# 14 of 49 node tiles of a top-1 expert layer through slots sorted by expert, and gathers handed out by a count of TensorE's work

## The chip, the cores and the metric

The kernel runs on one core of one Trainium2 chip. The metric is the device time of one execution in microseconds (us). The kernel before was timed 11 times: median 2865.29 us, from 2860.51 to 2869.4. The profile shows one execution more.

## What is computed

There are 6250 nodes with 256 features and 100,000 weighted edges, sorted by destination. Each of two layers has a part that adds over edges (gnn) and a part of experts (ffn), and each part adds its result to x. In layer 0 every node goes through all 8 experts, weighted by a softmax. In layer 1 each node goes through one of 32 experts only:

```python
x = x + L0_gnn(layernorm(x)); x = x + L0_ffn(layernorm(x))
# L1_gnn
h = layernorm(x) @ weight                      # 256 x 256
x = x + segment_sum(edge_val * h[edge_src], edge_dst) + bias
# L1_ffn, xf = layernorm(x)
idx = argmax(xf @ router_w.T + router_b)       # one of 32 experts for each node
h = relu(xf @ W1[idx] + b1[idx])               # 256 -> 64
x = x + relu(h @ W2[idx] + b2[idx])            # 64 -> 256
```

All of it is float32. x stays in SBUF, as 49 tiles of 128 nodes (X).

## The kernel before, in words

**Stages.** First the edges are sorted (to about 390 us); then comes layer 0 with its dense experts, and from about 1797 us layer 1. The change is in layer 1, apart from one fill in layer 0.

**Columns.** Edges are worked off in columns of 128. Layer 1 has 782, of which the first 64 (NE) are already done at the end of layer 0; 718 are left. `columns1` gives, for a column, a gather of 128 rows of h1 from DRAM (`gather`, L201, an indirect DMA that POOL issues), a scaling on ACT (L230) and a remainder on DVE (L231) into a tile m, a one-hot matrix s of destinations for three columns on DVE (L222), and one matmul that adds the column into its destinations (L277). Every 16 columns a tile of nodes is complete: its sums are put together on DVE, turned on PE (L209) and multiplied by the weight (L214), and added to X (L215). That takes up to LAG = 10 more steps of the generator. Buffers: 23 for gathered rows, 12 for m, 5 for s.

**Dense experts of layer 1.** The tiles are taken in blocks: 3, then 11 blocks of 4, then 2. `begin1` normalizes and turns a block's tiles (L340), computes the router (L973) and a mask that is negative and huge for every expert but the node's own. Two experts make a chunk of 128 hidden features, so there are 16 chunks. `hidden1` multiplies the turned block by a chunk of W1 (L1000) and adds the mask (L1003); ACT applies the relu (L1005). `outs1` multiplies by the chunk of W2 and adds up in PSUM (L1016). So every node goes through all 32 experts, and 31 of its results are zero. `end1` adds the result to X and writes the block (L1023, L1027).

**Order.** The order is written out by hand. A block can begin when all columns of its tiles are summed. `Stream.upto` emits columns up to a given number; `aheads` spreads them evenly over the half chunks, so that the columns of the next block are done some chunks before it begins. The engines work through their own queues in order and wait on semaphores.

**Layer 0, for the fill.** `small1` runs in the third last block of layer 0, at about 1525 us. It loads the router's weights and biases; b2 is loaded from SP into b2f, a tile with one buffer (tag hs), and split on DVE into three parts in bf16 (L803 to L809).

Of the kernel before, what the change touches and what calls it, by code (L numbers as in the profile page):

```python
# [11 lines left out]
I32 = mybir.dt.int32  # L12
# [32 lines left out]
LN_EPS = 1e-5  # L45
BN_EPS = 1e-3
# [3 lines left out]
def gnn_ffn_kernel(ctx: ExitStack, tc: tile.TileContext, a, out):  # L50
# [40 lines left out]
    h1 = dram.tile([NT * P, D], F32, name="h1")  # L91

# [143 lines left out]
    def columns1(pool, psum, js, h, idx, w, bufs):  # L236
# [6 lines left out]
        def summed(q, acc):  # L243
# [15 lines left out]
            else:  # L259
# [3 lines left out]
                sT = pool.tile([P, 2, P], F32, tag="sT", name="sT", bufs=2)  # L263
# [96 lines left out]
    ramp = [3] + [NB] * 11 + [2]  # L360
    blocks1 = [list(range(sum(ramp[:b]), sum(ramp[:b + 1]))) for b in range(len(ramp))]
# [273 lines left out]
    with tc.tile_pool(name="layer0", bufs=1) as wp, tc.tile_pool(name="outs0", bufs=1, side="right") as wo_pool, \  # L635
# [159 lines left out]
        def small1():  # L795


            nc.sync.dma_start(rw, a["router_t"].rearrange("(k p) e -> p k e", p=P))
# [150 lines left out]
        for part in firsts:  # L949
            next(part)  # L950
# [5 lines left out]
    with tc.tile_pool(name="layer1", bufs=1, reuse_waits="tile") as wp, \  # L956
# [8 lines left out]
        def begin1(pool, tiles):  # L965

            n = len(tiles)
            nw = n * P
            nT = norm_t(pool, psum, tiles)
            pl = psum.tile([P, NB, NX1], F32, tag="tr", name="pl", bufs=1)  # L970
            for j in range(n):
                for k in range(2):
                    nc.tensor.matmul(pl[:, j, :], nT[:, k, j * P:(j + 1) * P], rw[:, k, :],  # L973
                                     start=(k == 0), stop=(k == 1))
# [9 lines left out]
            nc.vector.tensor_tensor(g, g, m[:, :, None].to_broadcast([P, n, NX1]), OP.is_equal)  # L984
            hots = work.tile([P, NB, P // NX1, NX1], F32, tag="hots", name="hots", bufs=1)
# [10 lines left out]
        def hidden1(pool, block, c):  # L996
# [7 lines left out]
            hm = pool.tile([P, NB * P], F32, tag="hm", name="hm", bufs=4)  # L1004
# [14 lines left out]
        def end1(pool, tiles, py):  # L1019
            n = len(tiles)  # L1020
            o = pool.tile([P, NB, D], F32, tag="hs", name="o", bufs=2)
            for j, t in enumerate(tiles):
                nc.vector.scalar_tensor_tensor(o[:, j, :], py[:, j, :], 0.0, X[:, t, :], op0=OP.max, op1=OP.add)  # L1023
            t = tiles[0]
            m = min(N - t * P, n * P) // P
            if m:
                nc.sync.dma_start(out[t * P:(t + m) * P, :].rearrange("(t p) d -> p t d", p=P), o[:, :m, :])  # L1027
            if m < n:
                nc.sync.dma_start(out[(t + m) * P:, :], o[:NLAST, m, :])

        with tc.tile_pool(name="flow1", bufs=1, reuse_waits="tile") as flow:

            sums = Stream(columns1(flow, psum, range(NE, NREAL), h1, src_c, val_c, (5, EW + 6, 12, 4)))
            cum = [0] + [min(CS * (2 * tiles[-1] + 2) + CS // 2, NREAL) + LAG - NE for tiles in blocks1[1:]]
# [91 lines left out]
```

## Time and profile before

| | |
|---|---|
| the profiled execution's own time | 2863.55 us |
| its span, first to last instruction | 2861.8 us |
| granted TensorE clock, mean | 0.975 |
| busy: PE, PEld, DVE, ACT, POOL | 2654.3, 1728.1, 1993.6, 1601.3, 1883.9 us |
| gathers of layer 1 (L201, src_c) | 718, issued from 1792.8 to 2741.8 us |
| the last column's matmul (L277) begins | 2784.8 us |
| the last matmul (L1016) | in a group from 2852.61 us |
| the last DMA is issued (L1029) | 2855.46 us |

Busy times are sums over an engine's instructions. Lines of a timeline give the start, the duration, engine, source line and operation, and in brackets how long the engine was idle before and what ended it. A line of a table by stretches gives the busy time and the number of instructions of PE, PEld, DVE, ACT and POOL in this order, then the granted clock, the share of the DMA engines and GB/s. PE is TensorE's matmuls, PEld its loads of weights, DVE VectorE, ACT ScalarE, POOL GpSimd, SP SyncE; a name with q is the engine's sequencer, which issues DMAs too. A float32 matmul of the program is two instructions in the trace.

### The profile page before, as it was taken

The numbers are of one execution on the slowest core, as the hardware profiler recorded it, in microseconds if no ns is written. First come the engines' busy times: TensorE is split into PE (matmuls) and PEld (weight loads), VectorE is DVE, ScalarE is ACT, GpSimd is POOL, SyncE is SP. The second block draws the span as 40 slices with busy tenths as digits, with TensorE's granted clock in tenths as the row PEclk, the third lists the DMA queues.
The fourth block names the chain that finished last, engine by engine and source line by source line (L and its number), as shares of the span: only waits on it lengthen the run. The fifth ranks groups of instructions, "written<-read, shape, count | busy, mean of one in ns | idle before, by whom it ended". The sixth has DMA issues, their size and how long they took to land.

```text
span 2861.8 us, 36648 instructions
## 1 busy us (share of the span) xinstructions
PE 2654.3 (93%) x10178; PEld 1728.1 (60%) x10238; DVE 1993.6 (70%) x4968; ACT 1601.3 (56%) x3741; POOL 1883.9 (66%) x1883
## 2 busy tenths in 40 slices
PE   5888848899999999999999998889999999999998
PEld 2444426765666666666666665556666666666666
DVE  8999987788868777766756646566666666666630
ACT  7777737655555555555554545455555555555532
POOL 4666657777766666666665526777777777777720
PEclk9999978999999999999999999899999999999999
DMA  4000033333333233233332214233333333333310
GB/s 152 19 19 19 19 135 97 102 102 101 92 97 93 86 100 93 84 96 96 94 86 78 84 41 147 86 106 102 105 109 109 107 108 103 106 107 109 109 43 12
DMA packets 120835, 254.30 MB, mean 89 GB/s; under 512 B 31477, under 2 KB 68169, under 8 KB 120617
## 3 DMA queue, kind: packets, MB, share of 16 engines
q0 software_dynamic: 77520, 211.78, 25.7%
q1 hardware_dynamic: 31672, 32.42, 3.4%
q10 hardware_dynamic: 11424, 7.63, 0.8%
q8 instruction: 84, 1.38, 0.2%
q14 instruction: 135, 1.10, 0.1%
HBM read 232.48 MB, written 19.25 MB: 88 GB/s over the span
## 4 chain that ended last, share of the span: by engine, by line
PE 63%; DMA 8%; DVE 6%; issue 6%; ACT 2%; POOL 1%; ACTq 0%; POOLq 0%; DVEq 0%; another core or an unknown queue 0%
PE ph L764 19%; PE py L776 10%; PE py L1016 9%; PE ph L1000 9%; PE acc L707 5%; PE acc L277 5%; DMA g<-h,src_c 4%; DMA g<-h,idx 3%; DVE m L231 1%; ACT m L230 1%; POOL g L201 1%; PE ph L214 1%; PE tr L340 1%; PE ph L1003 1%; PE pl L973 1%
## 5 line engine op out<-in xcount | busy, mean ns | idle before, releaser
L201 POOL DMA_INDIRECT g<-h,idx x833 | 858.2, 1030 | 397.3 <-DVE m L231 195.5
L201 POOL DMA_INDIRECT g<-h,src_c x718 | 728.7, 1015 | 233.8 <-issue 103.0
L230 ACT ACTIVATE m<-g,w 128x256 fp32r<-128x256 f32 x833 | 370.8, 500 | 259.8 <-PE acc L707 161.4
L230 ACT ACTIVATE m<-g,val_c 128x256 fp32r<-128x256 f32 x718 | 348.2, 503 | 269.8 <-PE acc L277 142.3
L767 ACT ACTIVATE hT<-ph,shift,scale 128x512 f32<-128x512 f32 (+3 forms) x480 | 329.3, 696 | 292.8 <-PE ph L764 284.7
L231 DVE SCALAR_TENSOR_TENSOR m<-g,val_c,m 128x256 fp32r<-128x256 f32 x718 | 336.3, 483 | 206.3 <-ACT m L230 202.1
L231 DVE SCALAR_TENSOR_TENSOR m<-g,w,m 128x256 fp32r<-128x256 f32 x833 | 377.7, 477 | 28.7 <-ACT m L230 27.9
L764 PE MATMUL ph<-nT,w 128*128 128x512 f32 (+3 forms) x960 | 374.8, 526 | 20.4 <-ACT hT L767 20.2
L1016 PE MATMUL py<-w,hm 128*128 128x256 f32 x1568 | 385.8, 384 | 2.4 <-ACT hm L1005 2.2
L776 PE MATMUL py<-wo,hT 128*128 128x256 f32 x1568 | 377.8, 385 | 7.2 <-DVE X L778 4.6
L1000 PE MATMUL ph<-nT,w 128*128 128x512 f32 (+2 forms) x832 | 378.9, 576 | 0.0
L764 PE MATMUL ph<-hT,w 128*128 128x512 f32 (+3 forms) x960 | 366.8, 517 | 0.7 <-ACT hT L767 0.7
L707 PE MATMUL acc<-m,s 128*128 128x512 f32 x833 | 313.6, 482 | 38.8 <-DVE scale L663 27.6
L776 PEld LDWEIGHTS py<-wo,hT 128*128 128x128 f32 x1568 | 291.9, 191 | 75.5 <-DVE X L778 22.0
L277 PE MATMUL acc<-m,s 128*128 128x512 f32 x782 | 333.2, 500 | 1.2 <-DVE m L231 1.2
L1016 PEld LDWEIGHTS py<-w,hm 128*128 128x128 f32 x1568 | 291.4, 193 | 52.4 <-ACT hm L1005 4.3
L222 DVE TENSOR_TENSOR s<-col,dl 128x384 fp32r<-128x384 f32 (+1 forms) x294 | 155.0, 528 | 194.8 <-PE acc L707 194.4
L764 PEld LDWEIGHTS ph<-nT,w 128*128 128x128 f32 x960 | 174.1, 196 | 166.5 <-issue 116.5
L1005 ACT ACTIVATE hm<-ph,b 128x512 f32<-128x512 f32 (+2 forms) x208 | 136.9, 659 | 208.3 <-PE ph L1003 152.3
L764 PEld LDWEIGHTS ph<-hT,w 128*128 128x128 f32 x960 | 174.8, 191 | 121.4 <-issue 91.9
L707 PEld LDWEIGHTS acc<-m,s 128*128 128x128 f32 x833 | 159.7, 195 | 104.2 <-issue 50.9
L1000 PEld LDWEIGHTS ph<-nT,w 128*128 128x128 f32 x832 | 158.7, 193 | 102.2 <-issue 81.8
(254 smaller groups left out, 3341.2 us busy)
## 6 DMA issues: line engine op xcount, KB each, us to landing
g<-h,idx POOLq DMA_INDIRECT x833, 2.8
g<-h,src_c POOLq DMA_INDIRECT x718, 2.8
h<-hs SPq DMA_DIRECT2D x25, 256.0 KB, 2.1
X<-in_x_dram SPq DMA_DIRECT2D x12, 512.0 KB, 8.2
out_dram<-o SPq DMA_DIRECT2D x11, 512.0 KB, 3.4
h<-hs SPq DMA_DIRECT2D x9, 512.0 KB, 3.0
w<-in_L_ffn_W_dram ACTq DMA_DIRECT2D x2, 2048.0 KB, 7.9
wo<-in_L_ffn_Wo_dram ACTq DMA_DIRECT2D x1, 2048.0 KB
```

The lines of the kernel that those rows point to most:

```text
L201: nc.gpsimd.indirect_dma_start(out=g, out_offset=None, in_=h, in_offset=bass.IndirectOffsetOnAxis(ap=idx, axis=0))
L222: nc.vector.tensor_tensor(s[:, :n], col[:, None, :].to_broadcast([P, n, P]), dl[:, j:j + n, None].to_broadcast([P, n, P]), OP.is_equal)
L230: nc.scalar.activation(m[:, 0, :], g, AF.Copy, scale=w)
L231: nc.vector.scalar_tensor_tensor(m[:, 1, :], g, w, m[:, 0, :], op0=OP.mult, op1=OP.subtract)
L277: nc.tensor.matmul(acc, s[:, (j - js.start) % SJ, :], m, start=opens, stop=done)
L707: nc.tensor.matmul(acc, s[:, j % SJ, :], m, start=(j == 0), stop=(j == EW - 1))
L764: nc.tensor.matmul(ph[:, :nw], (w1, w2)[layer][:, e, k, m * P:(m + 1) * P], src[:, k, :nw], start=(k == 0), stop=(k == 1))
L767: nc.scalar.activation(hT[:, m, :nw], ph[:, :nw], AF.Relu, bias=shift[:, layer, c:c + 1], scale=scale[:, layer, c:c + 1])
L776: nc.tensor.matmul(py, hT[:, k, j * P:(j + 1) * P], wo[:, e, k, :], start=(k == 0), stop=(k == 1))
L1000: nc.tensor.matmul(ph[:, :nw], w1f[:, k, c * P:(c + 1) * P], nT[:, k, :nw], start=(k == 0), stop=False)
L1005: nc.scalar.activation(hm[:, :nw], ph[:, :nw], AF.Relu, bias=b1[:, c:c + 1])
L1016: nc.tensor.matmul(py[:, j, :], now[:, cols], w2f[:, c, :], start=False, stop=(c == NC1 - 1), skip_group_check=True)
```

## The change

**Routed tiles.** 14 tiles (7, 8, 13 to 15, 20 to 22, 27 to 29, 34, 39, 40) are no longer in dense blocks. The dense blocks are now 0 to 2; 3 to 6; 9 to 12; 16 to 19; 23 to 26; 30 to 33; 35 to 38; 41 to 43; 44 and 45; 46 and 47; 48. When a group of routed tiles is summed, `begin_routed` normalizes it, computes the router, and counts each node's rank within its expert. After tile 40, `slots` gives every node a slot: each expert has whole units of 64 slots, and two units make a pair of 128 rows. `scatter` writes the normalized rows into xs in DRAM by slot, an indirect DMA for each tile. Then, for each of NU = 30 pairs, `fetch` reads from SP the two experts' numbers into registers and loads their weights (wa, wb, each in two transfers) and 128 rows of xs (xt); `turn` transposes xt, `inside` and `outside` do the two products, and the result goes to ys in DRAM. At the end `finish` gathers each routed tile's rows from ys and adds them to X.

**Columns by a count.** `pace` adds up PE's work in units of one gather (HALF_CHUNK for a tile and half a chunk, COLUMN for a column, UNIT_WORK for a pair) and emits as many columns as units have passed. When the next dense block needs more columns than that, they are emitted at once.

**Smaller edits.** The gathers have 18 buffers and m has 9, s 4 and hm 3. `small1` fills xs with zeros. `end1` writes each tile by itself.

```diff
+UNIT = 64
+HALF_CHUNK = 0.37
+COLUMN = 0.24
+UNIT_WORK = 1.0
+BEHIND = 2
+ROUTED = [[7, 8], [13, 14, 15], [20, 21, 22], [27, 28, 29], [34], [39, 40]]
+LAST = [3, 2, 2, 1]
+KR = sum(len(r) for r in ROUTED)
+NU = -(-(KR * P // UNIT + NX1 - 1) // 2)
...
         def small1():
+            zero = wp.tile([P, D], F32, tag="hs", name="zero", bufs=1)
+            nc.vector.memset(zero, 0.0)
+            nc.sync.dma_start(xs.rearrange("(t p) d -> p t d", p=P), zero[:, None, :].to_broadcast([P, NU, D]))
...
-            sums = Stream(columns1(flow, psum, range(NE, NREAL), h1, src_c, val_c, (5, EW + 6, 12, 4)))
-            cum = [0] + [min(CS * (2 * tiles[-1] + 2) + CS // 2, NREAL) + LAG - NE for tiles in blocks1[1:]]
-            plans = aheads(cum, 2 * NC1, [4] + [8] * (len(blocks1) - 1))
+            sums = Stream(columns1(flow, psum, range(NE, NREAL), h1, src_c, val_c, (4, 18, 9, 4)))
+            def summed_at(t):
+                return min(CS * (2 * t + 2) + CS // 2, NREAL) + LAG - NE
+            def due():
+                return Pace.now - Pace.others - BEHIND
+            def pace(work, least=0):
+                Pace.now += work
+                n = min(max(least, int(due())), NREAL - NE + LAG)
+                if n > sums.at:
+                    Pace.now = max(Pace.now + COLUMN * (n - sums.at), n + Pace.others + BEHIND)
+                    sums.upto(n)
...
+            def scatter(j):
+                row = flow.tile([P, D], F32, tag="xt", name="row", bufs=3)
+                nc.vector.tensor_scalar(row, X[:, routed[j], :], normal[:, j, 0:1], normal[:, j, 1:2],
+                                        op0=OP.subtract, op1=OP.mult)
+                nc.gpsimd.indirect_dma_start(out=xs, out_offset=bass.IndirectOffsetOnAxis(ap=slot[:, j:j + 1], axis=0),
+                                             in_=row, in_offset=None)
+            def fetch(i):
+                wa = flow.tile([P, 2, 2, UNIT], F32, tag="wa", name="wa", bufs=3)
+                wb = flow.tile([P, 2 * D + 1], F32, tag="wb", name="wb", bufs=3)
+                for u in range(2):
+                    e = nc.values_load(unit_of[0:1, 2 * i + u:2 * i + u + 1], engines=(mybir.EngineType.SP,),
...
+                    nc.sync.dma_start(wa[:, :, u, :], a["w1_u"][bass.ds(e * P, P), :].rearrange("p (k h) -> p k h", k=2))
+                    nc.sync.dma_start(wb[u * UNIT:(u + 1) * UNIT, :], a["w2_u"][bass.ds(e * UNIT, UNIT), :])
+                xt = flow.tile([P, D], F32, tag="xt", name="xt", bufs=3)
+                nc.sync.dma_start(xt, xs[i * P:(i + 1) * P, :])
+                held[i] = [wa, wb, xt]
+            def turn(i):
+                xT = flow.tile([P, 2, P], F32, tag="sT", name="xT", bufs=4)
+                transposed(psum, held[i][2], xT)
+            def inside(i):
+                wa, wb, _, xT = held[i]
+                ph = psum.tile([P, P], F32, tag="mm", name="ph", bufs=3)
+                for k in range(2):
+                    nc.tensor.matmul(ph, wa[:, k].rearrange("p u h -> p (u h)"), xT[:, k, :], start=(k == 0), stop=(k == 1))
+                for u in range(2):
+                    us = slice(u * UNIT, (u + 1) * UNIT)
+                    nc.scalar.activation(inner[i % 3][us, us], ph[us, us], AF.Relu, bias=wb[us, D:D + 1])
+            def outside(i):
+                wb = held.pop(i)[1]
+                py = psum.tile([P, D], F32, tag="mm", name="py", bufs=3)
+                nc.tensor.matmul(py, inner[i % 3], wb[:, :D], start=True, stop=True)
+                y = flow.tile([P, D], F32, tag="o", name="y", bufs=5)
+                nc.vector.tensor_tensor(y, py, wb[:, D + 1:], OP.add)
+                nc.sync.dma_start(ys[i * P:(i + 1) * P, :], y)
+            def finish(j):
+                g = gather(flow, ys, slot[:, j:j + 1], 18)
+                nc.vector.scalar_tensor_tensor(g, g, 0.0, X[:, routed[j], :], op0=OP.max, op1=OP.add)
+                nc.sync.dma_start(out[routed[j] * P:(routed[j] + 1) * P, :], g)
+            def experts():
+                slots()
+                done_at = sums.at
+                for j in range(KR):
+                    while sums.at < done_at + LAG + j:
+                        yield
+                    scatter(j)
+                    Pace.others += 1
+                for i in range(3):
+                    fetch(i)
+                while sums.at < done_at + 2 * LAG + KR:
+                    yield
+                for i in range(-1, NU + 1):
+                    if 3 <= i + 3 < NU:
+                        fetch(i + 3)
+                    if i > 0:
+                        outside(i - 1)
+                    if 0 <= i < NU:
+                        inside(i)
+                    if i + 1 < NU:
+                        turn(i + 1)
+                    pace(UNIT_WORK)
+                    yield
...
                 for c in range(NC1):
-                    sums.upto(plans[b][2 * c])
+                    pace(n * HALF_CHUNK)
+                    while waiting and sums.at >= summed_at(waiting[0][-1]):
+                        tiles_r = waiting.pop(0)
+                        begin_routed(routed.index(tiles_r[0]), tiles_r)
+                    if not waiting:
+                        fill = fill or experts()
+                        next(fill, None)
...
-                    sums.upto(plans[b][2 * c + 1])
+                    pace(n * HALF_CHUNK)
...
+                    if fill:
+                        next(fill, None)
                     outs1(mine, c, now, py, n)
-                    if c == NC1 - (3 if b == 0 else 5) and not last:
-                        after = begin1(flow, blocks1[b + 1])
+                    if c >= NC1 - (3 if b == 0 else 5) and not last and after is None:
+                        need = summed_at(blocks1[b + 1][-1])
+                        if due() >= need or c == NC1 - 2:
+                            pace(0, need)
+                            after = begin1(flow, blocks1[b + 1])
+                if last:
+                    for _ in fill:
+                        pass
+                    for j in range(KR):
+                        finish(j)
```

## The prediction

> **What bounds the kernel now.** I read the busy time by stretches of the span first, then the lines of POOL, the timelines of POOL and PE, and the chain. Layer 1 begins at about 1797 us. From there PE is 77 to 100% busy, and POOL shows 77%, in every stretch the same:
>
> ```profile
> 2300.00:2400.00 100.00, 99.92 (x393) 69.18 (x399) 65.52 (x155) 54.12 (x120) 76.54 (x78) 1.00 0.37 106
> 2600.00:2700.00 100.00, 99.87 (x394) 68.38 (x400) 65.26 (x156) 53.72 (x121) 76.55 (x78) 1.00 0.39 112
> ```
>
> The 77% is a full POOL. Its timeline shows gathers of 0.95 us, each 0.30 us after the one before, and no longer gap from the second to the last:
>
> ```profile
> 1796.85 0.94 POOL L201 DMA_INDIRECT g<-h,src_c  x1 [3.12 <-PE acc L277]
> ...
> 2303.01 0.95 POOL L201 DMA_INDIRECT g<-h,src_c  x1 [0.30 <-DVE mv L330]
> 2304.26 0.95 POOL L201 DMA_INDIRECT g<-h,src_c  x1 [0.30 <-DVE m L231]
> ...
> 2741.84 0.95 POOL L201 DMA_INDIRECT g<-h,src_c  x1 [0.30 <-DVE rstd L332]
> ```
>
> ```profile
> L201 POOL DMA_INDIRECT g<-h,src_c x718 | 728.7, 1015 | 233.8 <-issue 103.0 <-DVE m L231 50.9 <-DVE s L222 16.4
> ```
>
> So 716 steps take 2741.84 - 1796.85 = 945 us, **1.32 us a column** (1.25 at the shortest). The idle time of the group, 233.8 us, is 718 gaps of 0.30 and two waits at the start. Columns can't come faster than this, whatever PE does.
>
> The chain names PE:
>
> ```profile
> PE 63%; DMA 8%; DVE 6%; issue 6%; ACT 2%; POOL 1%; ACTq 0%; POOLq 0%; DVEq 0%; another core or an unknown queue 0%
> ```
>
> In layer 1 both are nearly full. PE's price list, from one chunk of a block of four tiles with four columns and one with none:
>
> ```profile
> 2302.78 1.88 PE L1000 MATMUL ph<-nT,w 128*128 128x512 f32 x4
> 2304.49 0.38 PE L1003 MATMUL ph<-cold,sel 128*128 128x512 bf16 x1
> 2304.52 0.82 PE L277 MATMUL acc<-m,s 128*128 128x512 f32 x2
> 2305.17 1.89 PE L1016 MATMUL py<-w,hm 128*128 128x256 f32 x8
> 2306.72 0.81 PE L277 MATMUL acc<-m,s 128*128 128x512 f32 x2
> 2307.37 1.88 PE L1000 MATMUL ph<-nT,w 128*128 128x512 f32 x4
> ...
> 2790.60 1.88 PE L1000 MATMUL ph<-nT,w 128*128 128x512 f32 x4
> 2792.32 0.38 PE L1003 MATMUL ph<-cold,sel 128*128 128x512 bf16 x1
> 2792.53 1.89 PE L1016 MATMUL py<-w,hm 128*128 128x256 f32 x8
> 2794.26 1.88 PE L1000 MATMUL ph<-nT,w 128*128 128x512 f32 x4
> ```
>
> Without columns a chunk takes 2794.26 - 2790.60 = 3.66 us, 0.915 a tile, so a dense tile is 16 x 0.915 = **14.6 us**. With four it takes 4.59, so a column is 0.93/4 = 0.23; its share of the product with the weight (L209 and L214, 1.08 us per 16 columns) makes it **0.30 us**.
>
> **Part 1, dense work taken out.** 14 tiles x 14.6 = 205 us of PE go, 30 pairs of units come. Where does it show? In the kernel before, a block of four spends 64 columns: POOL 64 x 1.32 = 84.5 us, PE 58.6 + 64 x 0.30 + 2 for its start = 80. The two are level, so PE has nothing to give away. In the changed kernel a block of four has, with its routed neighbours, 112 columns to wait for: POOL 148 us, PE 58.6 + 34 + 4 = 97. In three blocks PE waits about 50 us each, and in every other one up to tile 38 POOL is the later as well (80 columns: 106 against 87). None of this time comes back: POOL sets when each block starts. It is worth something only if less PE work is left when POOL is done with it.
>
> **Part 2, what is left for the end.** By the engines' orders of the changed kernel, the first turn of sorted rows (line 1169's transposes, from tile xt) stands on PE after 665 gathered columns, with 53 columns behind it. What PE has to do from there:
> - tiles 41 to 48, dense: 8 x 14.6 = 117 us
> - 30 pairs of units: two transposes 0.22, four passes of 128 columns at 0.11 (a 512 pass takes 0.43), two of 256 at 0.21: 1.1 us each, 33 us
> - 53 columns x 0.30 = 16 us; the starts of the last three blocks, 3 us
>
> Together **169 us**. In the kernel before, the 665th gather is issued at about 2672 and the span ends 190 us later. So the tail shrinks by some 20 us only; the time saved lies in the middle, where POOL hides it.
>
> **Part 3, the wait that takes its place.** That first turn needs xt, xt reads xs, and xs needs all 14 scatters. They stand on POOL among the gathers: 675 gathers and 14 scatters end before xt can be fetched, while PE needs only 665 + 11 POOL steps to stand there. No scatter is in this trace. Bounds: 0.95 us, a gather without its gap, and 2.0, the longest gather of layer 0; I take 1.32, a gather's step, as it has as many rows. Then step 689 is at 1796.85 + 687 x 1.32 = 2703.7; three memsets on POOL 1 us (the iota of L838 took 0.64); landing as a gather's, 2.8; issue and landing of xt 2.3. First turn at **2709.8**, some 18 us after PE stands there.
>
> **Part 4, the zero fill.** xs is filled in layer 0, in the call of small1 at about 1530 us: 3.84 MB from SP.
>
> ```profile
> h<-hs SPq DMA_DIRECT2D x25, 256.0 KB, 2.1
> ...
> h<-hs SPq DMA_DIRECT2D x9, 512.0 KB, 3.0
> ```
>
> That is 0.9 us per 256 KB, so 2.1 + 14 x 0.9 = 14.7 us. b2f uses the same buffer (tag hs, one buffer) and so waits for it on SP, then lands 3.4 us later, at 1548.4. Its copies stand on DVE after 11 other instructions, which by the trace end at 1541.4; DVE is then idle until 1547.3. With 2.6 us of copies DVE is 3.7 us late, and PE, 100% busy here, waits for DVE's sums. I take **4 us**; 0 if it is covered, 15 if the gathers halve the fill's rate. The Trainium skill, "DMA: Bandwidth & Descriptors", Anatomy of one DMA — SWDGE (gpsimd) path, fits 2.0 us + bytes/436e3 for transfers issued by GpSimd: 11 us for this one, and then the term would be 0; the rows above are slower, and decide.
>
> **Part 5, SP.** Per pair SP issues two register loads, four weight transfers, xt and the result. A register load on SP took 0.27 to 0.47 us, with 0.17 for its arithmetic; an issue about 0.42 (three of b2f took 1.27):
>
> ```profile
> L292 SPq TENSOR_LOAD <-badi x2: 273/370/468, 382.4 to 383.2; - x2
> ```
>
> 2 x 0.54 + 6 x 0.42 = 3.6 us a pair. 27 pairs are fetched after the first three, as buffers come free (three of each): 97 us, plus 9 for first release, landing and last pair, 106. PE's own work while the pairs run is 33 + 42 (block 41 to 43) + 16 + 3 = 94. I add **12 us**; bounds 0 and 40 (4.6 us a pair, if each waits for its buffer too).
>
> **At nothing:** the ranks and slots (small DVE and PE work; PE idles there), the 14 gathers of finish (18 us on POOL, beside the last dense blocks; uncovered, 18 us), fewer buffers (18 g, 9 m, where POOL waits for nobody).
>
> **Sum.** 2709.8 + 4 + 169 + 12 = 2894.8. From PE's last end to the span's end it was 2861.8 - 2854.5 = 7.3: span 2902.1. The execution's own time was 2863.55, 1.75 above its span: **2904 us**. The median of the runs, 2865.3, is 0.06% above the profiled execution; I leave that out.
>
> The Trainium skill, "TensorE: Matmul & The Clock Gate", What's actually happening (Part 1), puts PE at half clock after an idle window of 3.4 us. The trace has 0.83 granted at 1800 to 1850 with PE 76% busy. By that rule the 18 us wait would cost 2 us more behind it; waits under POOL cost nothing.
>
> **Rivals.**
> - *Tail without new waits.* Parts 4 and 5 hidden, and the scatters near their lower bound (14 x 0.37 = 5 us less): 2904 - 21 = 2883. For it: both terms rest on orders, not on rows. 20%.
> - *POOL steps faster.* With DVE's dense work thinner, the step falls from 1.32 towards 1.25, seen at 1798 to 1808, where DVE is quiet. That is 687 x 0.07 = 48 us: 2856. It decides from 1.26 downwards, and from 1.29 if parts 4 and 5 are hidden too. Against it: gathers are stretched mainly beside m and s (L231, L222), which come with every column and stay. 9%.
> - *SP, or the buffers, set the pace:* 4.6 us a pair, 2904 + 28 = 2932. For it: three buffers only, and SP takes every issue in order; against it: the weights of a pair need no result of the one before. 15%.
> - *It does not do what it says.* The count hands out four columns a chunk, 64 of a block's 112; the rest comes in one bunch because the next block needs it. Then the count decides nothing, as POOL does: the time is the forecast's.
>
> **Chances.** Forecast 56%. Same mechanism, all of it: 2866 (2883, and a step of 1.295: 687 x 0.025 = 17 less) to 2940 (2932, and a fill of 12 instead of 4); dear scatters (14 x 0.68 = 10 more) stay inside. Of the faster POOL's 9%, 7 are faster by over 0.2% (about what can be told from no change here) and 2 within it; 2 of the short tail's 20 are within 0.2% too. So faster 7%, same 4%, slower 89%.
>
> **What would show it.** POOL's step 1.3 to the end with 14 scatters in it; PE at 65% between 1900 and 2550; a PE wait of 15 to 20 us before the first turn at about 2714; pairs every 3.6 us or more; some 185 us from that turn to the end. Wrong if POOL's last gather is before 2745, or if PE has under 150 us left at that turn.

## The result and the profile after

The changed kernel takes **2974.64 us** (median of 8 runs, 2970.40 to 2980.86), the kernel before 2866.24 us beside it (31 runs): **1.0379 times**, 95% interval 1.037 to 1.0389. It is slower, as forecast, but by 108 us and not by 39, and it lies outside the range of 2866 to 2940. The profiled execution took 2970.38 us, its span is 2968.6 us against 2902.1 forecast: **66.5 us** to explain. Three of the chips used for the experiments take 11 to 12% longer for every kernel, the kernel before included (3170 to 3218 us); runs from there are set only against the kernel before on the same chip, and as the three kernels that ran on both kinds have ratios lower by 0.011 to 0.014 there, a ratio from there is not carried over to the others.

The same two stretches as before, and two of 50 us from one block (PE, PEld, DVE, ACT, POOL, each with its count; clock; share of DMA; GB/s):

```profile
2300.00:2400.00 100.00, 77.92 (x257) 50.88 (x260) 56.82 (x143) 43.48 (x96) 77.59 (x74) 0.78 0.35 102
2600.00:2700.00 100.00, 91.62 (x336) 60.86 (x339) 58.74 (x161) 44.19 (x99) 73.71 (x72) 0.92 0.37 107
2050.00:2100.00 50.00, 50.00 (x191) 34.83 (x194) 31.61 (x78) 25.84 (x59) 38.30 (x39) 1.00 0.35 101
2150.00:2200.00 50.00, 27.88 (x71) 16.85 (x72) 24.83 (x70) 17.12 (x40) 39.11 (x36) 0.56 0.36 106
```

POOL is about as busy as before, 74 to 78%, while PE in the first stretch is busy for a fifth less and runs a third fewer instructions (257 for 393). A block of four with three routed neighbours is full for its first half and starved in the second: 27.88 of 50 us busy, and those at a granted clock of 0.56, so that by the two together less than a third of a full PE is left (an estimate; 71 instructions for 191). But POOL has issued 36 gathers in the second stretch against 39 in the first. Its timeline, at a place where a bunch of columns is worked off, and the lines of DVE there:

```profile
2127.41 0.94 POOL L212 DMA_INDIRECT g<-h,src_c  x1 [0.30 <-DVE sums L262]
2128.65 4.62 POOL L212 DMA_INDIRECT g<-h,src_c  x1 [0.30 <-DVE m L242]
2133.58 0.94 POOL L212 DMA_INDIRECT g<-h,src_c  x1 [0.30 <-issue]
```

```profile
2128.60 0.54 DVE L233 TENSOR_TENSOR s<-col,dl_c 128x384 fp32r<-128x384 f32 x1
2129.07 1.26 DVE L242 SCALAR_TENSOR_TENSOR m<-g,val_c,m 128x256 fp32r<-128x256 f32 x3
2130.26 0.54 DVE L233 TENSOR_TENSOR s<-col,dl_c 128x384 fp32r<-128x384 f32 x1
2130.73 1.26 DVE L242 SCALAR_TENSOR_TENSOR m<-g,val_c,m 128x256 fp32r<-128x256 f32 x3
2131.91 0.54 DVE L233 TENSOR_TENSOR s<-col,dl_c 128x384 fp32r<-128x384 f32 x1
```

One gather takes 4.62 us instead of 0.95. None of the DVE lines has a bracket: DVE runs m and s without a gap, until 2132.45. The gather ends 0.8 us later. Six more such gathers, at 1999.65, 2152.56, 2281.70, 2305.73, 2434.38 and 2458.98, take over 4 us each, and all seven end 0.82 or 0.83 us behind such a stretch of DVE. Such a stretch alone is not enough, though: from 2046.87 to 2051.92 DVE runs without a bracket too, m and s among it, and the five gathers beside it take 0.94 to 0.96 us. What the difference is stays open. The kernel before has one gather over 4 us and one over 2 in all of layer 1, and the longer of them has the same picture, 0.8 us behind DVE's m and s:

```profile
1831.79 5.45 POOL L201 DMA_INDIRECT g<-h,src_c  x1 [0.30 <-DVE s L222]
```

The line of the group after the change:

```profile
L212 POOL DMA_INDIRECT g<-h,src_c x718 | 748.0, 1042 | 241.0 <-issue 107.1
```

1042 ns a gather instead of 1015. The chain names PE for 59% instead of 63%, DVE for 18% instead of 6%, and SP for the first time:

```profile
PE 59%; DVE 18%; DMA 10%; issue 6%; ACT 3%; POOL 2%; SPq 2%; ACTq 0%; POOLq 0%; DVEq 0%; another core or an unknown queue 0%
```

The first scatters on POOL (start, duration; in brackets the idle time before):

```profile
2666.78 1.01 POOL L1150 DMA_INDIRECT xs<-row,slot  x1 [0.30 <-issue]
2668.10 0.97 POOL L212 DMA_INDIRECT g<-h,src_c  x1 [0.30 <-issue]
2670.50 1.00 POOL L1150 DMA_INDIRECT xs<-row,slot  x1 [1.43 <-DMA xs<-row,slot]
2671.80 0.97 POOL L212 DMA_INDIRECT g<-h,src_c  x1 [0.30 <-issue]
2673.21 1.04 POOL L1150 DMA_INDIRECT xs<-row,slot  x1 [0.44 <-DMA xs<-row,slot]
```

and what DVE's normalisation of their rows waits for (us in total, times, longest):

```profile
DVE row L1148 <- DMA xs<-row,slot: 21.0, 8, 9.8
```

A scatter itself is a step like a gather, 1.0 us and a gap. But by its bracket POOL waits until the scatter before has landed: where they follow closely, it is 2.7 us from one scatter to the next. DVE waits for landings too, before it normalises the next rows. With the idle time before them the 14 scatters take 25.5 us of POOL, 1.82 each (ten 1.3 to 1.5, four 2.4 to 3.2). The first turn of the pairs on PE, and the last:

```profile
2741.01 0.66 PE L351 MATMUL tr<-ident,xt 128*128 128x128 f32 x2 [8.13 <-DMA xt<-xs]
...
2748.99 0.38 PE L351 MATMUL tr<-ident,xt 128*128 128x128 f32 x2
...
2878.30 0.41 PE L351 MATMUL tr<-ident,xt 128*128 128x128 f32 x2 [0.65 <-DMA xt<-xs]
```

137.3 us for 29 intervals, 4.73 us a pair. SP's queue in one of them:

```profile
2813.58 0.57 SPq L1162 DMA_DIRECT2D wa<-in_w_u_dram  x1
2814.40 0.50 SPq L1163 DMA_DIRECT2D wb<-in_w_u_dram  x1
2815.44 0.56 SPq L1162 DMA_DIRECT2D wa<-in_w_u_dram  x1
2816.20 0.49 SPq L1163 DMA_DIRECT2D wb<-in_w_u_dram  x1
2816.74 0.58 SPq L1165 DMA_DIRECT2D xt<-xs  x1
2817.37 0.42 SPq L1188 DMA_DIRECT2D ys<-y  x1
2818.39 0.57 SPq L1162 DMA_DIRECT2D wa<-in_w_u_dram  x1
```

From one pair's first issue to the next one's it is 4.81 us, and no line has a wait in brackets. What lies between the lines is the loading of a register and its arithmetic (0.54 to 0.60 ahead of each wa) and about 0.2 ahead of each wb. xt takes 0.58 us although its address is fixed.

The zero fill (KB, us to landing) took what the forecast worked out, 14.7:

```profile
xs<-zero SPq DMA_DIRECT2D x1, 3840.0 KB, 15.0
```

### The profile page after: what moved, and what is told of

It is laid out like the page before. It is cut to its first block, busy times and chain, and to the rows that moved or that the text cites. A ratio compares the mean times of both kernels' runs of the same rounds, so it can differ in the third digit from the quotient of the medians.

```text
span 2968.6 us, 36992 instructions
## 1 busy us (share of the span) xinstructions
PE 2575.4 (87%) x9831; PEld 1669.1 (56%) x9868; DVE 2004.3 (68%) x5108; ACT 1599.3 (54%) x3799; POOL 1933.4 (65%) x1914
## 3 DMA queue, kind: packets, MB, share of 16 engines
q8 instruction: 82, 1.34, 0.2%
## 4 chain that ended last, share of the span: by engine, by line
PE 59%; DVE 18%; DMA 10%; issue 6%; ACT 3%; POOL 2%; SPq 2%; ACTq 0%; POOLq 0%; DVEq 0%; another core or an unknown queue 0%
PE ph L781 20%; PE py L793 10%; PE ph L1026 7%; PE py L1042 7%; PE acc L724 5%; DMA g<-h,src_c 5%; PE acc L288 4%; DMA g<-h,idx 3%; DVE loads L544 3%; DVE to L540 2%; POOL g L212 2%; DVE m L242 2%; ACT m L241 1%; PE tr L351 1%; PE pl L991 1%
## 5 line engine op out<-in xcount | busy, mean ns | idle before, releaser
L212 POOL DMA_INDIRECT g<-h,src_c x718 | 748.0, 1042 | 241.0 <-issue 107.1
L241 ACT ACTIVATE m<-g,val_c 128x256 fp32r<-128x256 f32 x718 | 337.8, 503 | 307.3 <-DMA g<-h,src_c 156.6
L288 PE MATMUL acc<-m,s 128*128 128x512 f32 x782 | 356.6, 534 | 121.2 <-DVE m L242 103.5
L781 PE MATMUL ph<-nT,w 128*128 128x512 f32 (+3 forms) x960 | 374.9, 526 | 22.7 <-ACT hT L784 22.6
L242 DVE SCALAR_TENSOR_TENSOR m<-g,val_c,m 128x256 fp32r<-128x256 f32 x718 | 324.8, 479 | 71.4 <-ACT m L241 68.5
L724 PE MATMUL acc<-m,s 128*128 128x512 f32 x833 | 313.4, 482 | 37.9 <-DVE scale L680 27.7
L1026 PE MATMUL ph<-nT,w 128*128 128x512 f32 (+3 forms) x704 | 287.5, 530 | 0.0
L1042 PE MATMUL py<-w,hm 128*128 128x256 f32 x1120 | 283.1, 384 | 0.8 <-ACT hm L1031 0.7
L288 PEld LDWEIGHTS acc<-m,s 128*128 128x128 f32 x782 | 164.0, 212 | 212.9 <-DVE m L242 72.4
L781 PEld LDWEIGHTS ph<-nT,w 128*128 128x128 f32 x960 | 173.3, 195 | 169.5 <-issue 117.0
L1042 PEld LDWEIGHTS py<-w,hm 128*128 128x128 f32 x1120 | 204.4, 191 | 37.7 <-ACT hm L1031 4.2
L724 PEld LDWEIGHTS acc<-m,s 128*128 128x128 f32 x833 | 159.2, 194 | 103.5 <-issue 50.7
L795 DVE SCALAR_TENSOR_TENSOR X<-py,gate,X 128x256 f32<-128x256 f32 x392 | 187.4, 480 | 37.1 <-PE py L793 32.8
```

The source lines that it names most:

```text
L212: nc.gpsimd.indirect_dma_start(out=g, out_offset=None, in_=h, in_offset=bass.IndirectOffsetOnAxis(ap=idx, axis=0))
L241: nc.scalar.activation(m[:, 0, :], g, AF.Copy, scale=w)
L242: nc.vector.scalar_tensor_tensor(m[:, 1, :], g, w, m[:, 0, :], op0=OP.mult, op1=OP.subtract)
L288: nc.tensor.matmul(acc, s[:, (j - js.start) % SJ, :], m, start=opens, stop=done)
L724: nc.tensor.matmul(acc, s[:, j % SJ, :], m, start=(j == 0), stop=(j == EW - 1))
L781: nc.tensor.matmul(ph[:, :nw], (w1, w2)[layer][:, e, k, m * P:(m + 1) * P], src[:, k, :nw], start=(k == 0), stop=(k == 1))
```

## Experiments

**Two theories** stood after the result. The first: POOL sets the middle whatever PE has to do, the dense work that was taken out is worth next to nothing, and the 66 us are a longer column step where columns come in bunches, dear scatters, and SP's issues. The rival: PE's work and its waits set the time, and the routed path costs what it does because rows go through HBM and back.

### The pairs left out (no_pairs)

```diff
-                slots()
+                return
-                g = gather(flow, ys, slot[:, j:j + 1], 18)
-                nc.vector.scalar_tensor_tensor(g, g, 0.0, X[:, routed[j], :], op0=OP.max, op1=OP.add)
-                nc.sync.dma_start(out[...], g)
+                nc.sync.dma_start(out[...], X[:, routed[j], :])
```

> Leaves out what the routed tiles need besides their places: no slots, no scatters, no pairs, no finish; the 14 routed tiles go out without their experts. The dense blocks and the handing out of columns by the count stay. Theory (GpSimd's step sets the middle, and what follows the last column is the work left on TensorE): the last column is issued some 25 us earlier than in the changed kernel, since 14 scatters are gone, and the tail is the dense work left, some 90 us: 2840 to 2860, that is, only 5 to 25 us below the kernel before although 205 us of TensorE's work is gone. Rival (TensorE's work sets the time): some 200 us below the kernel before, 2665.

Measured: 2865.90 us, 1.001 times the kernel before (0.9996 to 1.0024). So 205 us of dense work can be left out, with only the routers and ranks of those tiles in its place, and the kernel is not measurably faster. The last gather is issued at

```profile
2767.66 1.14 POOL L212 DMA_INDIRECT g<-h,src_c  x1 [0.30 <-DVE sums L262]
```

that is 25.8 us later than in the kernel before (2741.84), though the same 718 gathers are all that POOL has to do. 4.6 us of it are a later start of layer 1; the idle time before the gathers is as before (234.4 us for 233.8), but the gathers themselves add up to 749.8 us instead of 728.7, and seven of them take over 4 us. Behind it follow 94 us instead of 120. The shorter tail and the slower POOL cancel. The rival of this run falls; the theory's own range, 2840 to 2860, is missed by 6 us. It also says what no repair of the routed path alone can beat while columns come in these bunches: 2866.

### Columns spread evenly (even)

```diff
-                    pace(n * HALF_CHUNK)
+                    sums.upto(plans[b][2 * c])
...
-                    pace(n * HALF_CHUNK)
+                    sums.upto(plans[b][2 * c + 1])
```

with `plans` from `aheads`, as in the kernel before, for the new blocks.

> The routed tiles stay, but layer 1's columns are spread evenly over the half chunks again, as in the kernel before, instead of by the count of work. Theory (a column step of GpSimd is longer, 1.43 us against 1.30, where the count leaves a bunch to the end of a block): the steps in the middle fall back to 1.30 to 1.33, column 643 is issued some 15 to 20 us earlier and the end moves with it, 2953 to 2962. Rival (GpSimd's longer step comes from the work of the routed tiles beside it, not from the bunching): within 5 us of the changed kernel.

Measured: 2991.29 us, 1.0439 (1.0422 to 1.0456), slower than the changed kernel. The step does what was expected, the time does not. The group's line is

```profile
L212 POOL DMA_INDIRECT g<-h,src_c x718 | 724.3, 1009 | 256.5 <-issue 102.4
```

1009 ns a gather against 1042, none over 4 us. Steps average 1.29 to 1.34 from the 37th to the 612th column; in the changed kernel the stretches that come in a bunch (columns 122 to 161, 219 to 273, 331 to 385, 443 to 497) average 1.43, those that are handed out by the count 1.30 to 1.32. The whole of the difference is the seven long gathers, one or two in each bunch: without them a gather in the bunches takes 1.005 us on average, and elsewhere 1.004. The 613th gather starts at 2608.0 instead of 2626.4, although layer 1 begins 4 us later: 22 us won with these 4, and the first turn comes at 2722.7 instead of 2741.0. Then it is lost: the pairs take as long as before (to 2862.1), but stand in earlier chunks, so that 127 us of dense work follow the last of them instead of 90. And the even plan gives out the last columns with the chunks, which the pairs hold up: POOL waits 26.7 us for DVE's m between 2640 and 2800. So bunching costs what the theory says up to the first turn; as a statement on the end it missed.

### The pairs' weights loaded three times only (weights_once)

```diff
-                wa = flow.tile(...); wb = flow.tile(...)
-                for u in range(2):
+                if i < 3: first_w[i] = (..., ...)
+                wa, wb = first_w[i % 3]
+                for u in range(2 if i < 3 else 0):
```

> The pairs after the third use the weights of the first three again, so 27 of 30 pairs load no register and fetch no weights (wrong experts for those rows); rows, matmuls and stores stay. Theory (the sequencer of SyncE sets the pace of the pairs with 3.6 to 4.8 us of loads and issues for each): the pairs fall from 4.8 us to 1.5 to 2.5 us each and the kernel is 60 to 90 us faster than the changed one, 2885 to 2915. Rival (the chain of one pair over three buffers, row in, turn, two products, store, sets the pace): the pairs stay above 4 us each and the time within 15 us of the changed one.

It leaves out the weight transfers of 27 pairs. Measured: 2932.53 us, 1.0231 (1.0214 to 1.0248): 42 us less than the changed kernel. The turns run from 2748.9 to 2843.5, 94.6 us or 3.26 a pair instead of 137.3. The saving of the pairs, 42.7 us, is the saving of the kernel. PE is 99% busy from 2750 to 2900: at 3.3 us a pair PE itself, with the chunks between the pairs, is the limit. That is why the expected 1.5 to 2.5 us a pair was too low.

### A second queue for the second unit (two_queues, two_queues_b)

```diff
+                    queue = (nc.sync, nc.scalar)[u]
-                    e = nc.values_load(..., engines=(mybir.EngineType.SP,),
+                    e = nc.values_load(..., engines=((mybir.EngineType.SP, mybir.EngineType.Activation)[u],),
-                    nc.sync.dma_start(wa[...]); nc.sync.dma_start(wb[...])
+                    queue.dma_start(wa[...]); queue.dma_start(wb[...])
```

> The second unit of every pair loads its register and starts its two weight transfers on ScalarE's queue instead of SyncE's; all else as in the changed kernel. Theory (SyncE's loads and issues set a pair's 4.8 us: 2 of 0.27, 2 of 0.57, 2 of 0.50, 0.58 and 0.42 us are 3.7 of them): SyncE is left some 2.3 to 3.3 us a pair, the 30 pairs take 100 us or less instead of 137, and the kernel is 25 to 42 us faster than the changed one (42 us is what leaving out 27 pairs' weights gave), 2933 to 2950. Rival (the transfers themselves or the three buffers set the pace, whoever starts them): within 8 us of the changed kernel. A second rival: the issues on ScalarE delay its own work and the time grows.

> The second unit of every pair loads its register and starts its two weight transfers on ScalarE's queue, as in two_queues, whose chip took 3218 us for the kernel before. Theory (SyncE's loads and issues set a pair's 4.8 us): the 30 pairs take about 105 us instead of 137 and the kernel 2935 to 2950, 1.024 to 1.030 times the kernel before. Rival (transfers or buffers set the pace): 2967 or more, 1.035 or more.

Measured: 2952.65 us, 1.0305 (1.0286 to 1.0324), 22 us less; on the slower chip 1.017 (1.0118 to 1.0222). All transfers are still made, and from the same buffers; only SP has less to issue, and the turns take 113.1 us, 3.90 a pair. So it is SP's issuing, not the transfers and not the three buffers, that set 4.8 us. The gain is 3 us short of the expected range. PE is 89% busy at 2750 to 2850, so it probably takes over as the limit before SP's 2.3 us are reached; no run shows that by itself.

### Row buffers of their own (rows_apart, rows_apart_b)

```diff
-                row = flow.tile([P, D], F32, tag="xt", name="row", bufs=3)
+                row = flow.tile([P, D], F32, tag="row", name="row", bufs=5)
```

> The rows that are scattered get five buffers of their own instead of sharing three with the rows that the pairs read. Theory (a row's normalisation waits for the scatter three before to land, and GpSimd waits for the row, so a scatter costs 2.0 to 2.7 us of GpSimd instead of one step of 1.3): the 14 scatters take 6 to 12 us less, the first turn and the end come as much earlier, 2962 to 2969. Rival (the first turn waits for something else, and the scatters only fill time that would be idle): within 4 us of the changed kernel.

> Five buffers of their own for the scattered rows, as in rows_apart. Theory (three buffers make a scatter cost 2.0 to 2.7 us): 6 to 12 us off the changed kernel, 2962 to 2969, if the first turn comes earlier by as much. Rival (the scatters' landing, not their buffers, paces them, or the pairs' loads move back to where they were): within 4 us, 2970 to 2979.

Measured: 2966.86 us, 1.035 (1.0332 to 1.0367), 8 us less (3.7 between the two profiled executions); on the slower chip 1.0239 (1.0199 to 1.028). The first turn is at 2735.4, 5.7 us earlier, and no longer waits for xt. The time is the theory's, its mechanism is not. The scatters follow each other as before and wait for the same landings:

```profile
2671.68 1.01 POOL L1150 DMA_INDIRECT xs<-row,slot  x1 [1.65 <-DMA xs<-row,slot]
2674.40 1.04 POOL L1150 DMA_INDIRECT xs<-row,slot  x1 [0.43 <-DMA xs<-row,slot]
2677.14 1.03 POOL L1150 DMA_INDIRECT xs<-row,slot  x1 [0.43 <-DMA xs<-row,slot]
```

DVE's rows still wait 20.2 us for them (8 times, 8.8 the longest), and the 14 scatters take 24.4 us of POOL instead of 25.5. What differs is that 30 gathers stand among the scatters instead of 32, some 2.6 us, and that the gather of 3.32 us at 2698.09 has no counterpart. So the 8 us are not shown to be the buffers'.

### Fewer and earlier tiles (early)

```diff
-ROUTED = [[7, 8], [13, 14, 15], [20, 21, 22], [27, 28, 29], [34], [39, 40]]
-LAST = [3, 2, 2, 1]
+ROUTED = [[7, 8], [13, 14], [19, 20], [25, 26]]
+LAST = [4, 4, 4, 4, 3, 2, 1]
```

> The routed tiles are chosen from the first half: 8 instead of 14, tiles 7 8, 13 14, 19 20 and 25 26, so that slots, scatters and pairs run while GpSimd is still gathering; the dense blocks after them are of 4, 4, 4, 4, 3, 2 and 1 tiles. Theory (what counts is the work on TensorE left when the last column is in; pairs under GpSimd's gathers cost nothing): the last column some 2755 to 2785 and a tail of 60 to 90 us, 2820 to 2870, at or below the kernel before. Rival (the routed machinery costs its time wherever it stands, since it delays GpSimd or the vector engine by as much): 2900 or more.

Measured: 2925.41 us, 1.0212 (1.0195 to 1.0229): the rival's number. The last gather comes at 2773.6, as the theory said, but 146 us follow it and not 60 to 90. The pairs run from 2444 to 2546, under the gathers, and yet the time is not won. PE is starved while the routed tiles are gathered, with a granted clock of 0.81 to 0.83, and full once they are over:

```profile
2100.00:2200.00 100.00, 79.39 (x283) 52.62 (x282) 60.11 (x149) 48.62 (x109) 77.14 (x76) 0.83 0.36 104
2200.00:2300.00 100.00, 80.61 (x291) 52.98 (x290) 63.96 (x170) 49.43 (x113) 76.54 (x78) 0.83 0.37 106
...
2600.00:2700.00 100.00, 100.00 (x401) 69.23 (x400) 64.97 (x157) 53.40 (x120) 75.91 (x78) 1.00 0.38 108
2700.00:2800.00 100.00, 100.00 (x399) 68.99 (x398) 62.79 (x153) 50.91 (x114) 64.30 (x64) 1.00 0.35 102
```

Dense work taken out early is time PE spends waiting; the work of the later blocks can't be drawn forward into it, for their columns are not gathered. From 1900 to 2600 PE is idle for 111 us, in the kernel before for 19. Eight tiles less are 117 us of dense work.

### One pair a chunk, and the repairs together (one_each, even_all, even_all_b, mixed, mixed_b)

one_each yields twice after each pair, so that a pair stands in every chunk instead of two. even_all is even, one_each, rows_apart and two_queues in one. mixed is even_all with the count instead of the even plan from the sorting of the slots on, and

```diff
-                while sums.at < done_at + 2 * LAG + KR:
+                while sums.at < done_at + 4 * LAG + KR:
```

> One pair for each chunk of a dense block instead of two, so that the 30 pairs lie beside 30 chunks and not 15. Theory (while SyncE sets 4.8 us a pair, TensorE has room for a second chunk beside each pair, and this dense work is then not left behind the pairs): some 15 chunks of two or three tiles, 1.8 to 2.7 us each, come off the tail, 20 to 40 us faster than the changed kernel, 2935 to 2955. Rival (TensorE has no room, or the pairs wait behind the chunks' own waits): within 8 us or slower.

> Four edits at once: columns spread evenly, one pair a chunk, rows in five buffers of their own, and the second unit's weights on ScalarE's queue. Theory: the last column comes at 2755 to 2775, pairs no longer hold up TensorE, and what is left is the dense work: 2870 to 2900, so even with these repaired not below the kernel before, since leaving out the whole of the pairs gave 2866. Rival (a wait not named yet holds the pairs or the first turn): 2930 or more.

> Even columns, one pair a chunk, five row buffers and two queues together, as in even_all. Theory: the bunching's 17 us, the pairs' pace and the tail left behind them go; 2875 to 2905, still above the kernel before, since leaving out the whole of the pairs gave no less than 2866. Rival (pairs spread over twice as many chunks end later than the dense work and hold the end): 2930 or more.

> All 14 tiles routed; columns spread evenly until the slots are sorted and by the count after that, one pair a chunk, five row buffers, two queues, and the first turn 20 columns later. Theory (the even plan hands out the last columns with chunks that the pairs hold up, and the 19.5 us at the first turn stand in the time; without both the parts add up): 2952 of two queues alone, less 17 to 22 for the bunching, 8 for the row buffers and 8 for the turn: 2895 to 2925, still above the kernel before. Rival (the routed rows' way through HBM and back holds TensorE whatever the order): 2945 or more.

> mixed once more, for the same reason. Theory (the first turn's wait and the even plan's late last columns are what held even_all at 2955): 2895 to 2930. Rival (the rows' way through HBM holds TensorE whatever the order): 2945 or more.

Measured: even_all 2955.40 us, 1.0316 (1.0295 to 1.0336), and 1.0189 (1.0137 to 1.0242) on a slower chip, far above the 2875 to 2905 expected. The reason can be read. First, with even columns PE comes to the first turn too early and stands there; then the pairs, spread over twice the chunks, hold up the chunks that carry the last columns:

```profile
2720.59 0.69 PE L351 MATMUL tr<-ident,xt 128*128 128x128 f32 x2 [19.50 <-DMA xt<-xs]
```

```profile
2750.06 0.95 POOL L212 DMA_INDIRECT g<-h,src_c  x1 [0.30 <-issue]
2794.89 1.02 POOL L212 DMA_INDIRECT g<-h,src_c  x1 [43.88 <-DVE m L242]
```

POOL stands 43.88 us, in which DVE does no m, and issues its last gather only at 2820.5, 22.5 us later than in the changed kernel. mixed repairs both, but ran only on slower chips: 1.0147 (1.0102 to 1.0191) and 1.0129 (1.0086 to 1.0172) of the kernel before there. Its order is the best of those with all 14 tiles by the ratios on such chips (two_queues 1.017, one_each 1.0183 with 1.0142 to 1.0225, even_all 1.0189), within intervals that overlap. Whether it would reach 2895 to 2930 where the kernel before takes 2866 is open: with the 0.011 to 0.014 by which ratios were lower on such chips it would be at about 2935 to 2947 (an estimate), above the theory's range. one_each ran only there, where the changed kernel did not; it is 18 us faster than rows_apart on the same chip, so its expected 20 to 40 us are not tested.

### The pairs left out, columns even (no_pairs_even)

The edits of no_pairs and even in one; it leaves out the same part as no_pairs.

> As no_pairs (leaves out slots, scatters, pairs and finish; the routed tiles go out without their experts), with the columns spread evenly. Theory (bunching makes a column step 1.43 us instead of 1.30, some 17 to 22 us over the middle): 2843 to 2855. Rival (what follows the last column on TensorE sets the end, so that earlier columns only make TensorE's queue longer): 2860 or more.

Measured, on a slower chip: 0.982 (0.9774 to 0.9865) of the kernel before. no_pairs is at 1.001 on another chip. The direction is the theory's (bunching took from no_pairs what its shorter tail gave), but the two are from different kinds of chips; with the 0.011 to 0.014 it would be at about 0.994 (an estimate), so it is likely but not shown to be below the kernel before.

### Few tiles, late (late4, late4_later, late5_later, late4_later_b)

```diff
+ROUTED = [[30], [34], [37], [40]]
+    for n in [3] + [4] * 6 + [3, 3, 2, 2, 2, 2, 2, 2]:
+        blocks1.append(dense[sum(len(b) for b in blocks1):][:n])
```

late4 also has the four edits of even_all, late4_later the later first turn as well; late5_later routes 26, 30, 33, 36 and 39.

> The same four edits, and only tiles 30, 34, 37 and 40 are routed, so that the blocks before them stay full and TensorE keeps its queue of work; blocks of 3, 3, 2, 2 and then 2 each. 20 pairs of some 1.1 us of TensorE take the place of 4 dense tiles of 14.6 us. Theory (in the kernel before both engines are full, and only a shorter queue of work at the last column can be gained): TensorE 58 - 22 = 36 us less work, GpSimd some 10 to 15 us later, 2835 to 2870, at or a little below the kernel before. Rival (each small block makes TensorE wait for GpSimd, so the gain is lost again): 2870 to 2900.

> late4 with the first turn of the pairs put 20 columns later in the order. In late4 TensorE stood 21.6 us at that turn, waiting for the rows to come back. Theory (TensorE is full from there to the end, so this wait stands in the time): 15 to 22 us less than late4, 2851 to 2858, below the kernel before. Rival (GpSimd's last column sets the end and TensorE would only wait elsewhere): 2868 or more.

> As late4_later, with five routed tiles, 26, 30, 33, 36 and 39, and a last block of one tile. One dense tile of 14.6 us less on TensorE, half a pair more. Theory: a further 5 to 14 us less than late4_later, 2840 to 2852. Rival (a routed tile that TensorE has no queue of work for makes it wait 14 us for GpSimd, which is all that the tile saved): within 5 us of late4_later or slower.

> late4_later once more; its chip took 3217 us for the kernel before, so it can't be set against late4, which ran where the kernel before takes 2868. Theory (the 21.6 us at the first turn stand in the time): 2850 to 2862, 0.994 to 0.998 times the kernel before. Rival (GpSimd's last column, or TensorE's work behind it, sets the end wherever the wait is put): 2868 to 2878.

Measured: late4 2873.00 us, 1.002 (1.0009 to 1.0031), the fastest that computes everything, and not below the kernel before. PE stays 94 to 100% busy to 2500; at 2654.4 it has stood 21.6 us at the first turn, and the last gather comes at 2770.7. Putting that turn later was to win this. It is not seen to: late4_later is at 1.0008 (0.9985 to 1.0032) and 1.0052 (1.0024 to 1.008), late5_later at 1.0022 (0.9996 to 1.0047), all on slower chips. In their traces the wait for xt is gone, and PE waits in other places instead (8, 20 and 31 us for DVE's normalised rows, xn, between 2800 and 3150). No version tried that computes everything is shown to be below the kernel before.

## Why the forecast was wrong

The direction and the mechanism were right; three prices were too low, and one of the rivals named the largest.

- **Part 1** held in its main point. POOL set when blocks start: from one block's first products to the next one's (L1036 at 2034.09, 2187.05, 2340.06 and 2493.48) it is 153.0, 153.0 and 153.4 us for 112 columns, where 148 was forecast. PE waited there, 36 us a block at a low clock instead of 50 at a full one: from 1900 to 2550 it was busy for 80% and not 65%, at a clock of 0.83. no_pairs shows what the 205 us of PE's work are worth: 26 us behind the last gather, and the later gathers take these back.
- **The step of 1.32 us in Parts 2 and 3** failed: the forecast took the mean step of the kernel before for columns that come in a bunch. Measured: 1.43 in the bunches, because of seven gathers of 4.1 to 4.8 us; the one of 5.45 us in the kernel before was the sign of it, and went into the mean. Gather 643 came at 2665.5, 21.8 us later than before, of which 4.9 are the later start: **+17 us**. Even columns brought the step to there back to 1.31. "The count decides nothing", as the last rival said, was wrong: it decides how DVE's work falls, and so POOL's step. The rival *POOL steps faster* went the wrong way.
- **Part 3, the scatters**, at 1.32 us each within bounds of 0.95 and 2.0, failed in the same direction: they took 1.82 on average, +7 us. The price of the instruction was right (1.03 us); what was missed is the wait for the landing of the scatter before. The 32 gathers between them took 1.41 us each, +3, and from the last scatter to the turn it was 4.6 us instead of 6.1: about **+9 us** at the first turn. The wait of PE at the first turn was 8.1 us and not 18, for PE came there late too. The first turn was at 2741.0, not 2713.8: 27 of the 66.5 us.
- **Part 4**: the sum came out, in part by luck. Layer 1 starts 4.9 us later, 4 was taken, and the fill took 15.0 us for 14.7. But the next store of layer 0 behind the fill is issued only 2.0 us later than before (1620.43 for 1618.48). The other 3 us arise between there and 1793, and that stretch takes 168.4 to 172.3 us in five runs whose kernels are alike up to there (168.8 in the kernel before). The Trainium skill, "DMA: Bandwidth & Descriptors", Anatomy of one DMA — SWDGE (gpsimd) path, gave 11 us by its fit for transfers issued by GpSimd; this transfer, issued by SP, took 4 us more than that fit, and the rows were the better guide.
- **Part 5** failed most. Its count of instructions was right and its price for a register load (0.54) too. An issue was priced at 0.42 us, from the three transfers of b2f; here wa takes 0.57 and wb 0.50 us with 0.2 us more ahead of wb, and xt 0.58. So the same eight instructions are 4.8 us and not 3.6: the pairs took 137 us, not 106: **+31 us**. That the address from a register is what makes them dearer is not shown: xt has a fixed one, and takes 0.58 us here and 0.32 in weights_once. *SP sets the pace* at 4.6 us, given 15%, was the case that came about, though not because each waits for its buffer: weights_once and two_queues show the issues.
- **Part 2** was nearly right. After the last turn 90.3 us remained where 82 was forecast: **+8 us**. 7 of them are the end of block 41 to 43 and the last pair, which the forecast had over by then: the first products of the next block come at 2885.36. From there the last five tiles take 76.4 us, where 5 x 14.6 and the starts were counted.

17 + 9 + 1 for the later start, and 31 + 8, are 66 us of the 66.5. The Trainium skill's rule on the clock ("TensorE: Matmul & The Clock Gate", What's actually happening (Part 1)), half clock after an idle window, fits what stands behind the wait at the first turn: two transposes take 0.66 us at 2741.0 and 0.38 at 2749.0, so PE ran slowly for a few microseconds (until about 2746.6), some 2 to 3 us lost in all by an estimate from these durations. What the forecast had said of it, that waits under POOL cost nothing, isn't contradicted: no_pairs has a clock of 0.73 to 0.93 in the stretches of 100 us from 1900 to 2600 and ends no later than the kernel before.

What stays open: why only some stretches of DVE hold a gather, what gave rows_apart its 8 us, how much of the first turn's wait is in the time once pairs and columns are ordered well (mixed, late4_later ran only on slower chips), and why those chips are slower. There POOL's steps average 1.56 to 1.66 us with gaps of up to 5 to 9 us, while the single gathers take as long as elsewhere (998 to 1038 ns on average).

## What to carry to other kernels

When two engines are level, taking work from one is worth only what it has left once the other is done: look at that moment, not at the sum of busy time. A change of order (here columns in bunches) can make the full engine slower as well, so price its step under the new order, not by the old mean, and look at the longest instructions behind that mean. And price the DMA issues on a queue each by its own kind: eight issues and loads, at a price taken from another transfer, came out a quarter too cheap, for each of 30 pairs.

## What the runs showed that was not expected

- A POOL gather can be held while DVE works without a gap: 4.62 us instead of 0.95 beside back-to-back m and s, seven of over 4 us in the changed kernel, none with even columns. All seven end 0.82 or 0.83 us behind DVE's stretch; but not every such stretch holds one.
- By the brackets an indirect scatter of this kernel starts only when the one before, into the same tensor, has landed: 2.7 us from one to the next, with three row buffers and with five.
- On SP a pair's issues took 0.57 us (wa), 0.50 (wb), 0.58 (xt) and 0.42 (ys); with the register's load and arithmetic it is 1.9 us for a unit of two transfers. xt falls to 0.32 us in weights_once, where it no longer stands beside wa and wb.
- PE's granted clock falls to 0.56 in stretches where it waits for POOL column by column, though it still is 28 of 50 us busy: its busy time is then no measure of its work. The same matmul of a column (L288) takes 684 ns there and 507 in the full stretch.
